# Block layouts in memory, a third weight buffer and a re-timed work order in a two-layer gated MLP with LoRA kernel

## The chip, the cores and the metric

The kernel runs on one NeuronCore of one Trainium2 chip. The metric is the device time of one execution in microseconds, and lower is better. A profiled execution gives a trace of every instruction on five engines: PE (TensorE, with its weight loads as PEld), DVE (VectorE), ACT (ScalarE), POOL (GpSimd) and SP (SyncE, which here only issues transfers).

## The reference, cut to what matters

The input `x` has shape (2, 1024, 256): two samples of 1024 tokens with 256 features. `cond` holds 8 router logits per sample.

```
rw = softmax(cond); w, sel = top_k(rw, 2); w = w / sum(w)       # two experts per sample
mlp(x; g, u, d) = (gelu(x @ g) * (x @ u)) @ d                   # g, u: 256 x 1024, d: 1024 x 256
x = x + sum_k w[k] * mlp(x; expert sel[k]) + mlp(x; shared)
x = x + x @ W_base.T + b_base + 2 * sum_e cond[e] * (x @ As[e].T) @ Bs[e].T
```

All of it is float32. Only the shared MLP and the two chosen experts of each sample are computed. The second layer's low-rank part is folded into one 256 x 256 matrix per sample before it is applied.

## The kernel before, in words

**Precision.** Each float32 operand is split into a rounded part (`hi_of`, a copy to fp32r) and the remainder (`lo_of`, a subtraction). A product is then three matmuls: hi*hi, lo*hi and hi*lo. This document calls the three a *triple*.

**Groups.** The work of the first layer is cut into 24 groups: sample `b` (2), MLP `s` (shared, then the two experts) and quarter `q` of the 1024 hidden columns. A group loads one weight tile `w_raw` of 128 x 1536 floats (768 KB): four gate-and-up blocks A11, A12, A22, A21, then the down weights. Tokens are handled in two blocks of 512. In group 0 the 2 x 2 x 2 block product is done in full (`plain_product`). All later groups use seven products, P1 to P7, instead of eight. The seven need sums of weight blocks (`weight_sum`, S1 to S4, on POOL, into the one buffer `sf`) and sums of `x` blocks (`x_sum`).

**A regular group.** On PE it is 22 triples: seven products each for gate and up, and eight half steps of the down product. PE accumulates in banks `ps_a*` and `ps_d*`. The products share these banks, so a partial result must be copied away before the next product may be added: ACT copies it (`keep`: r1 after P1, u2 after P6, u3 after P7, for g and u), and DVE forms sums from it (`add_part`). The results go through gelu (ACT), `times_up` (DVE), `act_hi` (ACT) and `act_lo` (DVE) into the down product. Meanwhile ACT and POOL prepare the next group's weights: "A hi" and "A1 lo", "A2 lo" (tile `wa`), "S hi" and "S lo" (tile `ws`), "D hi", "D0 lo" and "D1 lo" (tile `wd`).

**Order.** Nothing is scheduled at run time. Every step is entered in a plan with a time (`at`). A regular group's step has the time `REGULAR[name]` plus 22 per group (`reg`); `MOVED` shifts single entries by their number. The plan is sorted by time and issued in that order, so each engine receives its instructions as an in-order queue, and these tables alone decide who stands behind whom.

**Buffers and transfers.** `w_raw` is a ring of two buffers; group g+2 is loaded (`load_w`, plan name "load") into the buffer of group g. Loads of shared weights are issued by SP (L199). Loads of expert weights are indirect transfers issued by POOL (L201), because the row index depends on the router. SP also loads `x` (L253, four blocks of 256 KB per sample, rows of 2 KB that lie 8 KB apart), the first weight tile in four pieces (`load_first`, L210) and the residual (L400), and stores the output (L429). Every load into a buffer has to wait until its last reader is done. In groups 4 and 5 the low-rank matrix is formed in between (`weff_*`, L381), which adds work on POOL and ACT.

**Start.** PE first runs 44 small matmuls (`warm_up`, L437) that depend on no data, then group 0. DVE and ACT split the first `x` blocks and weight pieces as they land. DVE also forms the router's result and `x_sum` 1 to 3. POOL waits for the second weight tile and then begins the sums for group 1.

Of the kernel before, what the change touches and what calls it, by code (L numbers as in the profile page):

```python
# [42 lines left out]
F32 = mybir.dt.float32  # L43
# [7 lines left out]
P = 128  # L51
TB = 512
# [1 line left out]
SCALING = 2.0  # L54
PIECE = 2
REGULAR = {
    "P1g": -1.6, "S1": -1.0, "A hi": -1.0, "r1g": -0.8, "P2g": 1.5, "P1u": 1.8, "P6g": 2.2, "P2u": 2.7,
    "r1 added g": 2.8, "r1u": 3.4, "u2g": 3.6, "S2": 3.6, "gelu 00": 4.5, "P6u": 4.7, "u2u": 5.5,
    "r1 added u": 5.7, "S3": 5.8, "P7g": 8.2, "P5g": 8.4, "S4": 8.5, "act 00": 8.8, "u3g": 8.9,
    "P5g mix": 9.3, "P5u": 11.5, "P7u": 11.6, "S hi": 13.4, "u3 added g": 13.7, "A1 lo": 14.3, "u3u": 14.8,  # L60
    "load": 14.9, "gelu 11": 15.0, "S lo": 15.2, "P4g": 15.4, "u3 added u": 16.0, "act 11": 16.2,
    "P3g": 16.5, "u2 added g": 16.5, "P4u": 16.6, "P3u": 16.6, "hi 00": 16.7, "gelu 10": 17.0,
    "down 00 0": 17.6, "act 10": 19.8, "lo 00": 20.0, "A2 lo": 20.3, "D hi": 20.4, "hi 11": 20.6,
    "u2 added u": 21.9, "gelu 01": 22.3, "lo 11": 22.8, "act 01": 24.9, "hi 10": 25.8, "lo 10": 26.9,
    "down 00 1": 27.8, "down 10 0": 28.2, "down 11 0": 29.0, "D0 lo": 29.7, "down 10 1": 32.0, "hi 01": 32.1,
    "D1 lo": 33.0, "lo 01": 36.9, "down 11 1": 37.3, "down 01 0": 37.6, "down 01 1": 38.3,
}
MOVED = {
    3: -40.0, 16: -9.2, 17: -8.4, 32: -2.9, 33: 3.1, 53: 4.5, 59: 2.8, 60: 3.1, 61: 2.9, 81: 4.9, 86: -35.5,
    99: 4.9, 100: 5.4, 622: -4.7, 1583: 7.7, 1586: 9.9, 1598: 8.0, 1604: 2.6,  # L70
}
WARM = 44
LEN = 22
# [12 lines left out]


@with_exitstack
def moe_then_lora(ctx: ExitStack, tc: tile.TileContext, xT, cond, skill, shared, second, outT):
    nc = tc.nc  # L90
    C, NT = xT.shape
    B, E = cond.shape
    NC = C // P
    G2 = 2 * P
    PW = 4 * G2 + PIECE * C
    NPC = skill.shape[0] // (E * P)
    S = NT // B
    T = S // TB
    assert NC == 2 and T == 2

    sb = ctx.enter_context(tc.tile_pool(name="sb", bufs=1))
# [13 lines left out]
    def const(shape, dtype, name):  # L115
        return sb.tile(shape, dtype, name=name, tag=name)

    raw_ring = Ring(sb, 2, [P, PW], F32, "w_raw")
    wa_ring = Ring(sb, 2, [P, 2, 3 * G2], F32R, "wa")
    sf = const([P, 4 * G2], F32, "sf")  # L120
    ws_ring = Ring(sb, 2, [P, 2, 4 * G2], F32R, "ws")
# [8 lines left out]

    xa = {(b, t): const([P, NC, TB], F32, f"xa{b}{t}") if b < B - 1 else
          raw_ring.tiles[t][:, 0:NC * TB].rearrange("p (c n) -> p c n", c=NC)
          for b in range(B) for t in range(T)}
    bank = {(m, h): pp.tile([P, TB], F32, name=f"ps_{m}{'gu'[h]}", tag=f"{m}{h}")
            for m in "ad" for h in (0, 1)}
    y = [[pp.tile([P, TB], F32, name=f"y{t}{c}", tag=f"y{t}{c}") for c in range(NC)] for t in range(T)]

# [50 lines left out]
    raw, wa, ws, wd = {}, {}, {}, {}  # L188
# [18 lines left out]
    def load_first(lo, hi):  # L207
        if 0 not in raw:
            raw[0] = raw_ring.next()
        nc.sync.dma_start(out=raw[0][:, lo:hi], in_=shared[0:P, lo:hi])  # L210

    def ssum(i):
        return sf[:, i * G2:(i + 1) * G2]
# [34 lines left out]

    xraw, xs = {}, {}

    def load_x(b, k, j, eng=None):
        xraw[b, k, j] = xr_ring.next()
        (eng or nc.sync).dma_start(  # L253
            out=xraw[b, k, j], in_=xT[k * P:(k + 1) * P, (b * T + j) * TB:(b * T + j + 1) * TB]
        )

    def x_sum(b, i, eng):

# [56 lines left out]
    sums, ge, act, acts = {}, {}, {}, {}  # L315
# [32 lines left out]
    def down(g, ij, half):  # L348
# [4 lines left out]
        a, w = acts[g, ij], wd[g]  # L353
        parts = [(n, c) for n in range(3) for c in range(NC)]
        for n, c in parts[:3] if half == 0 else parts[3:]:
# [6 lines left out]
    lora = {}  # L362
    lin = const([P, (2 + NC) * C + B + NC], F32, "lora_in")
    As_sb, BsT_sb, wbT_sb = lin[:, 0:C], lin[:, C:2 * C], lin[:, 2 * C:(2 + NC) * C]
    mix, bias_sb = lin[:, (2 + NC) * C:(2 + NC) * C + B], lin[:, (2 + NC) * C + B:]
# [30 lines left out]
    xres, xas = {}, {}  # L396

    def load_res(b, t, c):
        xres[b, t, c] = xr_ring.next()
        nc.sync.dma_start(out=xres[b, t, c],  # L400
                          in_=xT[c * P:(c + 1) * P, (b * T + t) * TB:(b * T + t + 1) * TB])

    def finish_y(b, t, c):
        nc.vector.tensor_tensor(xa[b, t][:, c, :], y[t][c], xres[b, t, c], ALU.add)
# [20 lines left out]
    def store(b, t, oc, n=slice(0, TB)):  # L425
        r = stores[(b * T + t) * NC + oc][:, n]
        nc.vector.scalar_tensor_tensor(r, outs[b, t, oc][:, n], bias_sb[:, oc:oc + 1],
                                       xa[b, t][:, oc, n], ALU.add, ALU.add)
        nc.sync.dma_start(  # L429
            out=outT[oc * P:(oc + 1) * P, (b * T + t) * TB:(b * T + t + 1) * TB][:, n], in_=r  # L430
        )


    def warm_up():
# [4 lines left out]
    V, A, G = nc.vector, nc.scalar, nc.gpsimd  # L439
# [49 lines left out]
    for n, ij in enumerate(((0, 0), (1, 0), (0, 1), (1, 1))):  # L489
        t = (2, 6, 10, 16)[n]  # L490
# [32 lines left out]
    for g in range(1, NG):  # L523
        if g + 2 < NG:
            reg(g, "load", load_w, g + 2)
        if g + 1 < NG:

            for i in range(4):
                reg(g, f"S{i + 1}", weight_sum, g + 1, i, G)
            reg(g, "S hi", split_ws, g + 1, 0, 4, hi_of, A)  # L530
            reg(g, "S lo", split_ws, g + 1, 0, 4, lo_of, V)
            reg(g, "A hi", split_wa, g + 1, 0, 3, hi_of, A)
# [13 lines left out]
        for ij in blocks:  # L546
            n = "%d%d" % ij
# [54 lines left out]
    b = B - 1  # L602
# [85 lines left out]
```

## Time and profile before

| What | us |
|---|---|
| Median of 3 runs (388.18 to 388.64) | 388.58 |
| The profiled execution's own time | 388.94 |
| Its span, first to last instruction | 387.2 |
| PE busy in the span (1706 matmuls) | 380.0 |
| DVE / ACT / POOL busy | 305.5 / 253.8 / 224.1 |
| First matmul of group 0 starts | 5.38 |
| Last matmul starts | 383.2 |

The span is 1.74 us shorter than the profiled execution's time; that rest lies outside the first and last instruction. The profiled execution is 0.36 us above the median. Matmuls overlap in the pipeline: a matmul of 512 columns is recorded with some 0.39 us, but in an undisturbed stretch they start 0.227 us apart, and a triple takes 0.68 us. The granted clock is 1.000 over the whole span.

### The profile page before, as it was taken

The page shows a single profiled execution, that of the slowest core. Times are in us where ns is not written, and L with a number is a line of the kernel's source. Part 1 is how long each engine was busy: PE and PEld are TensorE (multiplying, and loading weights), DVE is VectorE, ACT ScalarE, POOL GpSimd, SP SyncE. Part 2 cuts the span into 40 slices and gives each one's busy share as a digit, 9 for nine tenths or more (in the row PEclk, how much of TensorE's full clock was granted, in tenths as well). Part 3 has the DMA queues.
Part 4 walks back from the last instruction along what each step waited for, and adds up shares of the span by engine and source line. Part 5 has one row for each costly group of instructions (what it writes and reads, how often), then busy time and mean ns, then how long its engine had stood idle before and what let it go on. Part 6 is the DMA issues. An engine that isn't in the chain of part 4 may idle for free.

```text
span 387.2 us, 4871 instructions
## 1 busy us (share of the span) xinstructions
PE 380.0 (98%) x1706; PEld 313.8 (81%) x1706; DVE 305.5 (79%) x421; ACT 253.8 (66%) x439; POOL 224.1 (58%) x216
## 2 busy tenths in 40 slices
PE   9899999999999999999999999999999999999996
PEld 8677887878888888888888888888888888888885
DVE  4988987797887798988979878777867877777585
ACT  3588876766666677667767876766666775665520
POOL 1667777787866763853834956846747648621000
PEclk9999999999999999999999999999999999999999
DMA  7415202021022202302306022022022021000014
GB/s 208 147 20 226 78 5 81 3 81 50 33 81 81 81 4 81 107 30 108 110 0 190 3 81 81 3 81 81 2 81 82 2 81 48 36 0 0 2 55 163
DMA packets 7832, 26.01 MB, mean 67 GB/s; under 512 B 880, under 2 KB 1664, under 8 KB 7808
## 3 DMA queue, kind: packets, MB, share of 16 engines
q0 software_dynamic: 2336, 12.59, 10.4%
q1 hardware_dynamic: 5472, 13.11, 10.0%
q8 instruction: 13, 0.21, 0.2%
q14 instruction: 11, 0.09, 0.1%
HBM read 23.60 MB, written 2.10 MB: 66 GB/s over the span
## 4 chain that ended last, share of the span: by engine, by line
PE 93%; DVE 2%; DMA 2%; ACT 1%; SPq 1%; issue 0%; ACTq 0%
PE y L358 33%; PE ps_au L289 17%; PE ps_ag L289 17%; PE ps_dg L289 13%; PE ps_du L289 13%; DMA xr<-in_xT 2%; DVE act L334 0%; PE ps_dg L381 0%; SPq L210 0%; DVE wd L183 0%; ACT r_g L313 0%; DVE xr L265 0%; DVE x L183 0%; ACT ws L180 0%; DVE acts L183 0%
## 5 line engine op out<-in xcount | busy, mean ns | idle before, releaser
L358 PE MATMUL y<-acts,wd 128*128 128x512 f32 x576 | 150.3, 389 | 1.3 <-DVE acts L183 1.3
L358 PEld LDWEIGHTS y<-acts,wd 128*128 128x128 f32 x576 | 107.9, 188 | 24.0 <-DVE acts L183 1.7
L222 POOL TENSOR_TENSOR sf<-w_raw 128x256 f32<-128x256 f32 x46 | 37.3, 811 | 106.6 <-DVE ws L183 85.5
L183 DVE TENSOR_TENSOR acts<-act,acts 128x512 fp32r<-128x512 f32 x96 | 75.2, 785 | 14.2 <-ACT acts L180 14.1
L183 POOL TENSOR_TENSOR wa<-w_raw,wa 128x512 fp32r<-128x512 f32 (+1 forms) x46 | 65.1, 1419 | 0.4
L180 ACT CAST acts<-act 128x512 fp32r<-128x512 f32 x96 | 59.4, 619 | 8.2 <-DVE act L336 4.0
L319 DVE TENSOR_TENSOR c_g<-ps_dg,u_g 128x512 f32<-128x512 f32 x46 | 31.7, 690 | 41.6 <-PE ps_dg L289 40.4
L313 ACT COPY u_g<-ps_ag 128x512 f32<-128x512 f32 x46 | 27.0, 588 | 38.0 <-PE ps_ag L289 36.1
L183 POOL TENSOR_TENSOR wd<-w_raw,wd 128x256 fp32r<-128x256 f32 x44 | 43.3, 986 | 9.4 <-ACT wd L180 9.4
L336 DVE SCALAR_TENSOR_TENSOR act<-ge,gate_w,c_u 128x512 f32<-128x512 f32 x48 | 44.6, 929 | 2.9
L328 ACT ACTIVATE ge<-c_g 128x512 f32<-128x512 f32 x69 | 43.8, 634 | 1.7 <-DVE c_g L319 1.7
L289 PE MATMUL ps_ag<-x,ws 128*128 128x512 f32 x138 | 39.0, 391 | 1.3 <-ACT r_g L313 1.3
L289 PE MATMUL ps_au<-x,ws 128*128 128x512 f32 x138 | 38.8, 389 | 0.0
L289 PE MATMUL ps_au<-x,wa 128*128 128x512 f32 x138 | 38.8, 389 | 0.0
L289 PE MATMUL ps_dg<-x,ws 128*128 128x512 f32 x138 | 38.8, 389 | 0.0
L289 PE MATMUL ps_du<-x,ws 128*128 128x512 f32 x138 | 38.7, 389 | 0.0
L289 PE MATMUL ps_ag<-x,wa 128*128 128x512 f32 x138 | 38.7, 389 | 0.0
L313 ACT COPY u_u<-ps_au 128x512 f32<-128x512 f32 x46 | 26.8, 582 | 14.8 <-PE ps_au L289 14.5
L319 DVE TENSOR_TENSOR c_u<-ps_du,u_u 128x512 f32<-128x512 f32 x46 | 31.5, 685 | 2.4 <-ACT u_u L313 2.1
L289 PEld LDWEIGHTS ps_ag<-x,ws 128*128 128x128 f32 x138 | 25.7, 188 | 7.5 <-ACT r_g L313 2.2
L183 DVE TENSOR_TENSOR ws<-sf,ws 128x1024 fp32r<-128x1024 f32 (+1 forms) x24 | 31.3, 1306 | 0.7
L289 PEld LDWEIGHTS ps_au<-x,ws 128*128 128x128 f32 x138 | 25.9, 188 | 5.4
(102 smaller groups left out, 549.7 us busy)
## 6 DMA issues: line engine op xcount, KB each, us to landing
w_raw<-in_shared SPq DMA_DIRECT2D x7, 768.0 KB, 4.4
xr<-in_xT SPq DMA_DIRECT2D x16, 256.0 KB, 4.9
lora_in<-in_second SPq DMA_DIRECT2D x1, 514.0 KB, 5.3
w_raw<-in_shared SPq DMA_DIRECT2D x2, 256.0 KB, 5.7
outT<-u_g SPq DMA_DIRECT2D x2, 256.0 KB, 2.1
outT<-u_u SPq DMA_DIRECT2D x2, 256.0 KB, 2.1
outT<-ge SPq DMA_DIRECT2D x4, 128.0 KB, 1.9
w_raw<-in_shared SPq DMA_DIRECT2D x2, 128.0 KB, 3.3
```

What stands on the lines that cost most here:

```text
L180: (eng.copy if eng is nc.scalar else eng.tensor_copy)(pair[:, 0, :], src)
L183: eng.tensor_tensor(pair[:, 1, :], src, pair[:, 0, :].bitcast(F32), ALU.subtract)
L222: eng.tensor_tensor(ssum(i), a, b, op)
L289: nc.tensor.matmul(ps, lhsT=l, rhs=r, start=(start and n == 0), stop=(n == len(parts) - 1), skip_group_check=True)
L313: nc.scalar.copy(part[m, h], bank["a", h])
L319: nc.vector.tensor_tensor(sums[g, h, ij], bank["d", h], part[m, h], ALU.add)
L328: nc.scalar.activation(ge[g, ij], result(g, 0, ij), AF.Gelu_apprx_tanh)
L336: nc.vector.scalar_tensor_tensor(act[g, ij], ge[g, ij], gate_w[:, s - 1, b:b + 1], result(g, 1, ij), ALU.mult, ALU.mult)
L358: nc.tensor.matmul(y[j][c], lhsT=w[:, wp, o:o + P], rhs=a[:, ap, :], start=first and n == 0, stop=last and n == 2, skip_group_check=True)
```

## The change

The change has four parts.

1. *Layout.* `x` and the output lie in memory as contiguous blocks of 128 x 512 (256 KB each); before, they were cut from a 256 x 2048 matrix. The first weight tile's four pieces lie in memory one behind the other in an array of their own, `piece0`. The numbers and sizes of the transfers stay as they were.
2. *Buffers.* `w_raw` has three buffers. Group g+2 goes into the buffer that group g-1 had.
3. *Order.* All entries of `REGULAR` and most of `MOVED` have new values.
4. *First transfers.* By the new `MOVED` the first weight piece is issued ahead of the first `x` block.

```diff
 REGULAR = {
-    "P1g": -1.6, "S1": -1.0, "A hi": -1.0, "r1g": -0.8, "P2g": 1.5, "P1u": 1.8, "P6g": 2.2, "P2u": 2.7,
-    "r1 added g": 2.8, "r1u": 3.4, "u2g": 3.6, "S2": 3.6, "gelu 00": 4.5, "P6u": 4.7, "u2u": 5.5,
-    "r1 added u": 5.7, "S3": 5.8, "P7g": 8.2, "P5g": 8.4, "S4": 8.5, "act 00": 8.8, "u3g": 8.9,
...
+    "P1g": -3.4, "r1g": -1.5, "A hi": -1.1, "P2g": -0.3, "P1u": -0.2, "r1 added g": 0.6, "P6g": 1.8,
+    "S1": 2.7, "P2u": 3.4, "r1u": 3.9, "P6u": 4.2, "u2g": 4.3, "r1 added u": 4.8, "S2": 5.1, "P5g": 5.5,
+    "gelu 00": 5.8, "S3": 7.1, "S4": 7.1, "A1 lo": 7.1, "u2u": 7.6, "S hi": 9.0, "P7g": 9.1, "u3g": 9.7,
+    "act 00": 10.0, "P5g mix": 10.2, "hi 00": 10.8, "P7u": 11.5, "load": 12.1, "P5u": 12.5,
...
+    "lo 11": 19.1, "hi 10": 22.8, "D hi": 23.8, "down 00 1": 23.8, "lo 10": 24.3, "down 10 0": 25.3,
...
+    "lo 01": 34.6, "down 01 0": 35.2, "down 01 1": 35.6, "D0 lo": 36.0, "D1 lo": 40.8,
 }
 MOVED = {
-    3: -40.0, 16: -9.2, 17: -8.4, 32: -2.9, 33: 3.1, 53: 4.5, 59: 2.8, 60: 3.1, 61: 2.9, 81: 4.9, 86: -35.5,
-    99: 4.9, 100: 5.4, 622: -4.7, 1583: 7.7, 1586: 9.9, 1598: 8.0, 1604: 2.6,
+    20: -0.2, 37: 2.4, 38: 2.9, 39: 3.5, 45: -4.1, 74: -1.8, 80: -1.5, 81: 2.7, 86: -35.0, 89: 2.2, 99: 8.1,
+    100: 3.7, 1583: 5.5, 1598: 4.3, 1604: 4.6,
 }
...
-    raw_ring = Ring(sb, 2, [P, PW], F32, "w_raw")
+    raw_ring = Ring(sb, 3, [P, PW], F32, "w_raw")
...
-        nc.sync.dma_start(out=raw[0][:, lo:hi], in_=shared[0:P, lo:hi])
+        nc.sync.dma_start(out=raw[0][:, lo:hi], in_=piece0[lo * P:hi * P].rearrange("(p c) -> p c", p=P))
...
-        (eng or nc.sync).dma_start(
-            out=xraw[b, k, j], in_=xT[k * P:(k + 1) * P, (b * T + j) * TB:(b * T + j + 1) * TB]
-        )
+        nc.sync.dma_start(out=xraw[b, k, j], in_=x[b, j, k])
...
-        nc.sync.dma_start(
-            out=outT[oc * P:(oc + 1) * P, (b * T + t) * TB:(b * T + t + 1) * TB][:, n], in_=r
-        )
+        nc.sync.dma_start(out=outT[b, t, oc][:, n], in_=r)
...
-        "xT": np.ascontiguousarray(np.asarray(x).reshape(B * S, C).T),
+        "x": np.ascontiguousarray(np.asarray(x).reshape(B, T, TB, NC, P).transpose(0, 1, 3, 4, 2)),
...
+        "piece0": np.concatenate([shared[0, :, lo:hi].reshape(-1) for lo, hi in
+                                 ((0, G2), (G2, 2 * G2), (2 * G2, 4 * G2), (4 * G2, shared.shape[2]))]),
```

The residual load changes as `load_x` does (`in_=x[b, t, c]`). What the new tables do to the queues, where this document speaks of it:

- ACT, start: before, the casts of `x` for P5 and P6 and of two activations stood ahead of the first half of "S hi", and then came the gelu of block 11; now this order is: cast for P5 (`x_76`), `act_hi` of block 01, cast for P6 (`x_75`), first half of "S hi", gelu of block 11.
- DVE, start: the remainder of the first activation (`acts` block 00) now stands before the remainder of `wd`; before, it stood behind it and behind `x_sum` 2.
- PE, group 0: both halves of down 00 now come before the two plain products of block 11, and both halves of down 10 between P1g and P2g of group 1.
- ACT, every group: r1g now stands ahead of "A hi"; before, "A hi" stood ahead of r1g. Then come hi 10, "D hi" and r1u.
- POOL, every group: the load stands ahead of "D0 lo" and "D1 lo"; before, it stood behind them.

## The prediction, made before the changed kernel was run

> **What bounds the kernel now.** I read the windows view first: the busy time of each engine by stage, to see where PE is not full.
>
> ```profile
> 0.00:13.00 13.00, 12.23 (x76) 10.86 (x77) 7.26 (x15) 6.05 (x12) 1.51 (x7) 1.00 0.66 202
> 13.00:25.00 12.00, 10.63 (x46) 8.13 (x45) 11.10 (x22) 7.72 (x16) 7.93 (x7) 1.00 0.20 67
> 60.00:100.00 40.00, 38.67 (x174) 31.29 (x173) 32.71 (x39) 26.79 (x48) 30.36 (x29) 1.00 0.19 60
> 100.00:367.00 267.00, 267.00 (x1180) 221.08 (x1179) 209.61 (x286) 181.88 (x313) 156.70 (x149) 1.00 0.17 56
> ```
>
> The columns are PE, PEld, DVE, ACT, POOL. From 100 to 367 us PE is busy for 267.00 of 267 us, and triples follow each other at 0.68 us: nothing is to be had there, only lost. What can be had lies in the first 100 us. The chain of waits in order of time shows the places, because its steps should be 0.68 us apart:
>
> ```profile
> 65.37 0.68 PE ps_dg L289 x3
> 66.05 0.69 PE ps_au L289 x3
> 67.36 0.97 PE ps_ag L289 x3
> 68.33 0.69 PE ps_du L289 x3
> ...
> 82.86 0.71 PE ps_au L289 x3
> 84.25 0.96 PE ps_ag L289 x3
> ```
>
> From 66.05 to 67.36 it is 1.31 us, so 0.63 too much, and the next triple takes 0.97, so 0.29 too much: 0.9 us (the refill after a stop is about 0.11 of it). I took the starts of all matmuls in the trace and subtracted 0.227 us each. Left over are: at 14.75 us 1.56 (with refill), at 21.6 0.35, at 36.9 0.14, at 66.3 0.90, at 81.6 0.15, at 83.2 0.98. Sum 4.08 us: the ceiling of what order and buffers can give, unless PE starts earlier.
>
> *The first stall* (timeline of the start):
>
> ```profile
> 12.57 2.10 POOL L222 TENSOR_TENSOR sf<-w_raw 128x256 f32<-128x256 f32 x2 [10.31 <-DMA w_raw<-in_shared]
> 12.85 1.23 DVE L183 TENSOR_TENSOR wd<-w_raw,wd 128x512 fp32r<-128x512 f32 x1
> 14.00 1.23 DVE L265 TENSOR_TENSOR xr<-xr,xr 128x512 f32<-128x512 f32 x1
> 15.15 1.21 DVE L183 TENSOR_TENSOR acts<-act,acts 128x512 fp32r<-128x512 f32 x1
> 16.42 0.73 PE L358 MATMUL y<-acts,wd 128*128 128x512 f32 x2 [1.29 <-DVE acts L183]
> ```
>
> PE waits for the first activation's remainder, which is third in DVE's queue. The same DVE operations take 0.68 us before POOL begins at 12.57 and 1.2 afterwards: they start 0.60 apart alone and 1.15 beside POOL.
>
> *The two stalls of the low-rank groups* (first the timeline of POOL):
>
> ```profile
> 59.92 1.90 POOL L201 DMA_INDIRECT w_raw<-in_skill,idx  x1 [0.16 <-POOL wa L183]
> ```
>
> and the timeline of ACT:
>
> ```profile
> 65.99 0.83 ACT L180 CAST wa<-w_raw 128x768 fp32r<-128x768 f32 x1 [2.84 <-DMA w_raw<-in_skill,idx]
> 66.73 0.58 ACT L313 COPY r_g<-ps_ag 128x512 f32<-128x512 f32 x1
> ```
>
> The expert's weights are issued at 59.92 and land at 65.9. ACT's "A hi" waits for them, and r_g stands behind it on ACT. PE's P6g waits for r_g. At 82.9 it is the same. The list of waits confirms both causes:
>
> ```profile
> ACT wa L180 <- DMA w_raw<-in_skill,idx: 4.0, 2, 2.8
> PE ps_ag L289 <- ACT r_g L313: 1.3, 2, 0.7
> PE y L358 <- DVE acts L183: 1.3, 1, 1.3
> ```
>
> **Third buffer and r1g ahead of "A hi".** In a regular group the load no longer needs group g's D lo to be done. In POOL's new order it follows A1 lo, which needs "A hi", and that comes 1.4 to 2.2 us after the group's first product starts. So the load is issued some 4 us into a group. By the rows above it takes 1.9 plus about 4.2 us and has landed by 10 to 11 us, 4 us before the next group (14.96 us = 22 x 0.68) begins. In group 4 POOL first waits for the low-rank copy (about 7.6 us in) and adds L389 (1.3), so the load lands about 15 us in; the group is 15.7 long with L381, and "A hi" needs it 1.4 us after that. In addition r_g no longer stands behind that cast. So 0.90 and 0.98 go, from two causes, each enough by itself. The small one at 81.6 came from a DVE operation of 2.83 us beside four POOL operations in a row (0.15); with POOL's queue reordered I count it as gone. Sum -2.03.
>
> **Start of PE: nothing.** The 44 warm-up matmuls follow at 0.105 us from 0.77 and end at 5.38, exactly when group 0 starts; their number stays. The first piece now goes ahead of x, but both were there by 4.5 us (ACT's first cast 4.54, DVE's 4.23). If x comes 0.3 us later its cast still ends at 5.0.
>
> **The start's new order, worked through with before's landings.** DVE: act 00 at 10.45, x_sum 3 at 11.04, acts lo at 11.80 (ACT's cast ends at 11.78), P3's remainder at 12.4, then beside POOL wd's remainder 13.0 to 14.2. PE needs that at 14.51 (the third matmul of down 00, which starts at 14.06): the stall of 1.56 goes. What is late next: x_sum 1 at 14.15, act 10 at 15.3 to 15.95. PE now runs the whole of down 00 first and wants the bank that act 10 reads at 15.65: stall 0.37 + 0.11 = 0.48. Then the router (1.1 us on DVE, from 18.00 to 19.12 in the trace), acts lo 17.0, act 01 18.1, x_sum 2 18.7 to 19.4. ACT's cast for P6 waits for that and starts at 19.45, half of "S hi" at 19.97, and only then the gelu of block 11, 20.5 to 21.1. PE wants the bank it frees for P2g at 18.63 + 3 x 0.68 = 20.67: stall 0.48 + 0.11 = 0.59. So behind PE's wait stand P1u, P6g and all the rest. Before, P2g came at 22.04 after the same number of matmuls; now at 21.15. r_u on ACT then ends at 24.75 against 24.65 wanted: 0.15. From there to 40 us my steps along the queues leave each product 0.5 us or more, so the 0.14 at 36.9 goes. In group 2 the exp and gelu tables (3.0 us on ACT, 38.48 to 41.47 in the trace) now stand ahead of u2g, which then ends at 41.25 where PE wants P7g at 41.2: 0.10.
>
> So this part removes 1.56 + 0.35 + 0.14 = 2.05 and adds 0.48 + 0.59 + 0.15 + 0.10 = 1.32: -0.73.
>
> Here the Trainium skill is weighed, *SBUF — State Buffer*, "SBUF: two separate sides": the port pair of DVE and POOL is an exclusive lock, and the loser is blocked for the other's whole instruction. A POOL operation of 256 columns takes 0.74 us alone (66.05), so by the rule a DVE operation behind one would come every 0.60 + 0.74 = 1.34 us; the trace has 1.15. With 1.34 act 10 would be 0.4 us later and the first new stall 0.9 instead of 0.48. I take 1.15, which was measured at this very place.
>
> **Layout: nothing at the centre.** For it speaks the list of DMA issues:
>
> ```profile
> w_raw<-in_shared SPq DMA_DIRECT2D x7, 768.0 KB, 4.4
> xr<-in_xT SPq DMA_DIRECT2D x16, 256.0 KB, 4.9
> ```
>
> A third of the bytes takes longer. But most x blocks were issued in fours behind each other. In the packet records a 2 KB packet takes 84 ns at the median; in the first 10 us 764 of them have some 28 us more in all, because single ones take up to 551. Over 16 engines that is 1.8 us: the most that contiguous blocks can bring forward the landing of the second weights (12.5). But the contiguous 6 KB rows have such packets too (median 234 ns, mean 291 from 13 to 22 us), so the layout may not be their cause: lower bound nothing. The skill, *DMA: Bandwidth & Descriptors*, "Latency and other measured facts", has power-of-two row pitches slow at 2 MiB (164 GB/s) and above; at 512 KiB it has 207, near full. Here the pitch is 8 KiB, so by the rule nothing is gained; by the packets up to 1.8 us of landing. And an earlier landing of the second weights starts POOL earlier, beside more of DVE's queue: with x 1.4 us and POOL 1.7 us earlier, act 10 comes at 16.3 instead of 15.95, and P2g again at about 21.1. I take 0, range -1 to +0.4. Stores: the last one lands 1.5 us after its issue with 1 KB packets of 47 ns; same packets after, at most -0.2.
>
> **Regular groups: nothing, by cover.** With steps of ACT at 0.5 us (casts of 768 columns 0.74), r_g starts at 0.88 us, A hi 1.36, hi 10 2.1, D hi 2.6, r_u 3.1 to 3.7; P6u wants it at 7 x 0.68 = 4.76. Cover 1.0 us. P6g wants r_g (ends 1.47) at 2.04. D0 lo is wanted at 14.05 and done by about 7. DVE's sums each have 1 us or more.
>
> **Sum.** -2.03 - 0.73 = -2.76, about -2.8: 388.94 - 2.8 = 386.1 for a profiled execution. The one shown lies 0.36 above the median, so against the median 388.58 I predict 385.8.
>
> **Rivals.**
> - *The layout pays*: landings come forward without the collision, and the new stalls close too. The whole 4.08 goes: 384.5. For it: x at 9.35 us holds DVE for 0.72. Against: the pitch, and POOL. Chance 0.14.
> - *The start only moves its stalls*: DVE is busy 11.10 of 12 us from 13 to 25 in any order. The start gains nothing or loses up to 1: 386.6 to 387.6, or below 0.2% of gain if the low-rank stalls return in part. Chance 0.22 (0.15 faster, 0.07 same).
> - *The third buffer's load gets in the way*: SP can now issue the third weights at about 5 us instead of 14. If their packets mix with the second's (768 KB, 2.7 us at the 286 GB/s of the packet records from 30 to 36 us), POOL starts at up to 15.2 and A1 lo of group 1 (done 5.0 us after POOL's start by its rows, wanted at 18.9) is 1.3 us late: 387.1, up to 388 with what hangs on it. For: all share 16 engines. Against: one queue, landings in order of issue in the trace. Chance 0.06. (The buffers' part not happening is excluded: SP's new queue has the load into a third tile.)
> - *Slower*: a wait in every regular group. ACT's r_u has cover 1.0 us; if hi 10 or "A hi" ahead of it is late by more, P6u stops. Price: 0.2 us over the cover costs 0.31 with refill, times 22 groups = 6.8, minus 2.8 gained: 392.6. It decides from 1.0 us of lateness on; break-even is 0.13 us per group. Chance 0.08.
>
> **Numbers.** The main case has 0.50, range 385.2 to 386.6. A measurement of this kernel can tell 0.2% (0.78 us) from no change. Faster by more: 0.50 + 0.14 + 0.15 + 0.04 = 0.83; within: 0.07 + 0.02 + 0.01 = 0.10; slower: 0.07. The range goes from the ceiling (384.5) to a gain of 1 (387.6).
>
> **What would show it.** Right: matmul starts of 0.68 per triple through groups 4 and 5, and the indirect transfers landing about 4 us ahead of "A hi"; no stop at 14.75, small ones near 15.7 and 20.7; group 0 at 5.38. Wrong: idle PE between 100 and 367 us (the slower rival); P2g of group 1 not before 22 us (start only moved); POOL's first operation well before 11 us (layout) or after 13.5 (mixing).

## The result and the profile after

The changed kernel took 386.26 us (median, 385.94 to 386.7) against 388.61 us of the kernel before, run beside it: a ratio of 0.9942, interval 0.993 to 0.9954. The gain is 2.35 us; 2.8 were forecast, and 385.8 was predicted. The profiled execution is the fastest of its kernel, 385.94 us with a span of 384.2, so between the two profiled executions the gain is 3.00 us.

The windows view of the kernel after, with the same columns (PE, PEld, DVE, ACT, POOL, then the granted clock):

```profile
0.00:13.00 13.00, 12.23 (x75) 10.79 (x76) 7.56 (x15) 6.26 (x12) 2.64 (x8) 1.00 0.79 263
13.00:25.00 12.00, 12.00 (x52) 9.17 (x51) 11.97 (x25) 8.13 (x16) 7.71 (x7) 1.00 0.45 154
60.00:100.00 40.00, 39.63 (x181) 32.61 (x180) 33.93 (x39) 27.56 (x49) 32.94 (x32) 1.00 0.13 40
100.00:364.00 264.00, 264.00 (x1166) 218.63 (x1165) 217.88 (x283) 178.55 (x309) 137.01 (x146) 1.00 0.17 56
```

From 13 to 25 us PE now has work in all of the 12 us (10.63 before), and DVE is fuller still: 11.97 of 12 us (11.10 before). From 60 to 100 us only 0.37 us is idle (1.33 before). From 100 to 364 us PE is full, as before: the new order costs the regular groups nothing. Since matmul records overlap, stops of 0.1 or 0.2 us do not show in the busy time; the starts of the matmuls, further below, show them.

The list of waits is the short form of the same. Columns: who waited for whom, us in total, times, longest. Of the old entries for `r_g` (1.3 us) and for `acts` (1.3 us) none is left on PE; the first entry is the wait before the first warm-up matmul:

```profile
PE y L431 <- PEq L676: 0.8, 1, 0.8
PE ps_dg L286 <- DVE c_g L316: 0.4, 1, 0.4
```

The remaining wait of 0.4 us is found in the chain of waits at 79.5 us, where the triple after it takes 0.96 instead of 0.68:

```profile
79.54 0.69 DVE c_g L316
80.22 0.04 issue
80.27 0.96 PE ps_dg L286 x3
```

**One balance for all kernels.** I took the starts of all matmuls in each trace and added up what lies between neighbours beyond 0.227 us. The last matmul starts at the first one's start plus these sums plus 373.1 to 373.3 us (373.5 in r1g_first and two_buffers), so little else moves the end of PE. The sums of 4 to 8 us include spacing at half speed (see below). "Tail" is the span less the last start. The columns 4–8 to 100–365 are stretches of the span in us. Stops of 0.08 us from 8 to 14 us in layout_only and lora_moved have no column.

| Kernel | median us | ratio to before (interval) | first matmul | 4–8 | 14–30 | 30–60 | 60–100 | 100–365 | last starts | tail |
|---|---|---|---|---|---|---|---|---|---|---|
| before | 388.61 | | 5.38 | 0.50 | 1.91 | 0.14 | 2.03 | 0 | 383.20 | 4.0 |
| after | 386.26 | 0.9942 (0.993–0.9954) | 5.38 | 0.72 | 0.60 | 0 | 0.64 | 0 | 380.58 | 3.6 |
| layout_only | 389.1 | 1.0014 (1.0008–1.0021) | 5.32 | 1.42 | 1.64 | 0 | 1.73 | 0 | 383.34 | 3.8 |
| order_and_buffers | 387.13 | 0.9958 (0.9944–0.9972) | 6.10 | 0.15 | 1.72 | 0 | 0.64 | 0 | 381.86 | 3.7 |
| r1g_first | 387.19 | 0.9964 (0.9951–0.9977) | 5.03 | 0.69 | 1.81 | 0.15 | 0.23 | 0 | 381.46 | 3.9 |
| three_buffers | 388.79 | 1.0004 (0.9995–1.0012) | 5.04 | 0.79 | 1.91 | 0.15 | 1.71 | 0 | 382.76 | 3.9 |
| load_early | 391.35 | 1.0078 (1.0058–1.0098) | 5.38 | 0.59 | 1.77 | 1.08 | 0 | 2.91 | 384.87 | 3.9 |
| two_buffers | 395.72 | 1.0174 (1.0157–1.0192) | 4.84 | 1.06 | 0.57 | 0 | 7.56 | 2.66 | 390.18 | 3.8 |
| r1g_behind | 386.14 | 0.9931 (0.9918–0.9944) | 5.38 | 0.66 | 0.82 | 0 | 0.64 | 0.15 | 380.86 | 3.6 |
| lora_moved | 385.58 | 0.9918 (0.9904–0.9931) | 5.08 | 1.63 | 0.56 | 0 | 0 | 0 | 380.56 | 3.6 |
| start_freed | 385.9 | 0.9917 (0.9904–0.993) | 5.00 | 1.68 | 0 | 0.37 | 0.64 | 0 | 380.84 | 3.6 |
| logits_late | 384.92 | 0.9908 (0.9892–0.9923) | 4.89 | 0.69 | 0 | 0 | 0.65 | 0 | 379.32 | 3.6 |
| all_freed | 384.8 | 0.9892 (0.9878–0.9907) | 5.38 | 0.71 | 0 | 0.27 | 0 | 0 | 379.46 | 3.6 |
| layout_logits_late | 387.27 | 0.9969 (0.9957–0.9981) | 5.07 | 0.64 | 0.53 | 0.26 | 2.15 | 0 | 381.81 | 3.8 |

The sums belong to the one profiled execution, the medians to all of them. Where two kernels' intervals overlap, the difference of their medians is no more than a hint unless the executions themselves lie apart. Between before and after the balance closes: 4–8 us +0.22, 14–30 us -1.31, 30–60 us -0.14, 60–100 us -1.39, tail -0.38; together -3.00. Of the tail's -0.38 the layout alone gives 0.17 (3.96 to 3.79 in layout_only); the rest was not traced.

Names: "block 10" of `x` is the second `x` transfer, features 128 to 255 of the first 512 tokens; act, hi and lo with a block number are `times_up`, `act_hi` and `act_lo` of that block.

### The profile page after: what moved, and what is told of

It is laid out like the page before. It is cut to its first block, busy times and chain, and to the rows that moved or that the text cites. A ratio compares the mean times of both kernels' runs of the same rounds, so it can differ in the third digit from the quotient of the medians.

```text
span 384.2 us, 4886 instructions
## 1 busy us (share of the span) xinstructions
PE 379.7 (99%) x1706; PEld 314.2 (82%) x1706; DVE 315.8 (82%) x421; ACT 252.6 (66%) x439; POOL 206.6 (54%) x216
## 3 DMA queue, kind: packets, MB, share of 16 engines
q1 hardware_dynamic: 5472, 13.11, 9.8%
## 4 chain that ended last, share of the span: by engine, by line
PE 97%; DVE 2%; issue 1%; DVEq 0%
PE y L355 33%; PE ps_au L286 17%; PE ps_ag L286 17%; PE ps_dg L286 13%; PE ps_du L286 13%; PE y L431 1%; PE ps_ag L306 1%; PE ps_au L306 1%; PE ps_du L306 1%; PE ps_dg L306 1%; DVE act L333 1%; PE ps_dg L378 0%; DVE c_g L316 0%; DVE ws L182 0%; DVE c_u L316 0%
## 5 line engine op out<-in xcount | busy, mean ns | idle before, releaser
L355 PE MATMUL y<-acts,wd 128*128 128x512 f32 x576 | 153.8, 389 | 0.0
L182 DVE TENSOR_TENSOR acts<-act,acts 128x512 fp32r<-128x512 f32 x96 | 83.3, 869 | 6.1 <-ACT acts L179 5.8
L182 POOL TENSOR_TENSOR wa<-w_raw,wa 128x512 fp32r<-128x512 f32 (+1 forms) x46 | 52.3, 1136 | 31.0 <-ACT wa L179 22.6
L316 DVE TENSOR_TENSOR c_g<-ps_dg,u_g 128x512 f32<-128x512 f32 x46 | 31.7, 689 | 35.5 <-ACT u_g L310 19.4
L333 DVE SCALAR_TENSOR_TENSOR act<-ge,gate_w,c_u 128x512 f32<-128x512 f32 x48 | 49.1, 1023 | 2.8
L182 POOL TENSOR_TENSOR wd<-w_raw,wd 128x256 fp32r<-128x256 f32 x44 | 40.1, 930 | 11.5 <-ACT wd L179 11.0
L325 ACT ACTIVATE ge<-ps_ag 128x512 f32<-128x512 f32 x25 | 14.9, 597 | 33.1 <-PE ps_ag L286 32.5
L286 PEld LDWEIGHTS ps_dg<-x,ws 128*128 128x128 f32 x138 | 25.9, 188 | 5.5
```

Of the source, the lines that this page charges most:

```text
L182: eng.tensor_tensor(pair[:, 1, :], src, pair[:, 0, :].bitcast(F32), ALU.subtract)
L286: nc.tensor.matmul(ps, lhsT=l, rhs=r, start=(start and n == 0), stop=(n == len(parts) - 1), skip_group_check=True)
L316: nc.vector.tensor_tensor(sums[g, h, ij], bank["d", h], part[m, h], ALU.add)
L325: nc.scalar.activation(ge[g, ij], result(g, 0, ij), AF.Gelu_apprx_tanh)
L333: nc.vector.scalar_tensor_tensor(act[g, ij], ge[g, ij], gate_w[:, s - 1, b:b + 1], result(g, 1, ij), ALU.mult, ALU.mult)
L355: nc.tensor.matmul(y[j][c], lhsT=w[:, wp, o:o + P], rhs=a[:, ap, :], start=first and n == 0, stop=last and n == 2, skip_group_check=True)
```

## The experiments

The theory to be tested: the gain is 2.03 us from the low-rank groups, by two causes (the third buffer and r1g), 0.73 us from the start's order, and nothing from the layout. The rivals: the layout does it, or only one of the two causes does.

### The layout and the rest, taken apart

layout_only is the kernel before with the block layouts of `x`, output and first weights; order_and_buffers is the kernel after with the old ones.

```diff
# layout_only: before, with
+        nc.sync.dma_start(out=raw[0][:, lo:hi], in_=piece0[lo * P:hi * P].rearrange("(p c) -> p c", p=P))
+        nc.sync.dma_start(out=xraw[b, k, j], in_=x[b, j, k])
...
# order_and_buffers: after, without these
```

> The kernel before with the block layouts of x, output and first pieces alone; orders and two buffers as before. Theory (order and buffers bring the gain): the stop of PE near 14.75 us stays at 1.0 to 1.6 us, those near 66 and 83 us stay at 0.9 and 1.0; only the stores at the end are shorter, so the time falls by 0.0 to 0.5 us against before. Rival (the layout pays): x and first weights land 1 us or more earlier, DVE is ahead, the stop near 14.75 us shrinks below 0.6, and the time falls by 1 us or more.

> The changed kernel with the old layouts (x cut from the 256 x 2048 matrix, first pieces cut from the weight tile's rows). Theory: it keeps nearly all, 1.8 to 2.6 us below before, with stops of PE under 0.4 us each near 15.7 and 20.4 and the 0.6 near 79.5. Rival (the layout pays): 1 us or less below before, since the new order of the start counts on early landings and its stops near 15.7 and 20.7 grow to 0.5 and more each.

Measured: the layout alone is 0.5 us slower (389.1), which neither side expected. Order and buffers alone give 387.13, 1.5 us below before and between the two expectations, so beside them the layout is worth 0.87 us in the medians. The intervals of order_and_buffers and after just overlap, but all five executions of the one (386.77 to 387.38) lie above all four of the other (385.94 to 386.7). The layout's worth is not one number: its sign depends on what else is done.

Alone, the first blocks land early, but `x` block 10 lands later (7.52 us, in before 6.58), and PE waits for it. The list of waits of layout_only:

```profile
PE y L354 <- DVE acts L181: 1.4, 1, 1.4
PE ps_ag L305 <- DVE x L178: 1.2, 1, 1.2
PE ps_ag L285 <- ACT r_g L309: 1.0, 2, 0.6
```

The wait of 1.2 us for `x` is new; the other two are before's. In exchange later stops shrink a little, as the one near 83 us does by 0.28: PE comes to it 0.43 us later, but the transfer that it hangs on lands only 0.14 us later. And the tail is 0.2 us shorter: its stores land 2.0 and 1.7 us after issue, against 2.1 and 1.9.

Without the layout, the new order has a start that is far from the one I worked out. The waits of order_and_buffers, in its profiled execution, which is the slowest of its five:

```profile
PE ps_dg L289 <- ACT ge L328: 0.7, 1, 0.7
PE ps_ag L309 <- DVE x L180: 0.5, 1, 0.5
PE ps_dg L289 <- DVE c_g L319: 0.4, 1, 0.4
PE ps_du L309 <- DVE act L334: 0.3, 1, 0.3
```

The first `x` block lands at 5.50 us (3.64 in after, 4.21 in before), the third at 9.87 (8.14 in after) and the second weights at 13.11 (11.38 and 12.50). DVE's and ACT's queues run 0.6 to 1.3 us later than in after, and the stops at the start sum up to 1.72 us instead of 0.60. DVE's timeline in order_and_buffers shows one more loss, an operation on 2 columns that takes 1.09 us while POOL is busy (0.39 us in after):

```profile
16.71 1.09 DVE L156 TENSOR_TENSOR gap<-top 128x2 f32<-128x2 f32 x1
```

### The two causes of the low-rank stalls, one by one, from before

```diff
# r1g_first
-    ... "A hi": -1.0, "r1g": -0.8, ...
+    ... "A hi": -1.0, "r1g": -1.1, ...
# three_buffers
-    raw_ring = Ring(sb, 2, [P, PW], F32, "w_raw")
+    raw_ring = Ring(sb, 3, [P, PW], F32, "w_raw")
# load_early: three_buffers, and
-    "load": 14.9, ...
+    "load": 7.6, ...
```

> The kernel before with one number changed: r1g at -1.1, so that ACT's copy r_g stands ahead of the cast A hi in every group. Theory (each cause enough by itself): the transfer still lands at 65.9 and 82.8, the cast still waits for it, but P6g no longer waits: the stops near 66 and 83 us go, the time falls by 1.6 to 2.0 us. Rival (only the earlier landing helps, because what stands behind the cast is then late: gelu and r_u): the stops move to P6u and less than 0.6 us is gained.

> The kernel before with a third weight buffer and nothing else. Theory (POOL's queue, not the buffer, holds the load back: before shows the issue waiting 0.16 us for POOL's own cast and no longer): the indirect loads are issued near 59.9 and 76.8 us as before, the stops near 66 and 83 us stay, the time is within 0.4 us of before. Rival (the buffer was what held it): the stops go, 1.5 to 2 us less.

> The kernel before with three weight buffers and the load ahead of D0 lo in POOL's queue (plan time 7.6 instead of 14.9); r1g stays behind A hi. Theory: the two transfers land 3 us or more earlier, A hi waits no more, the stops near 66 and 83 us go, the time falls by 1.6 to 2.0 us. Rival (the landing was not the bound, POOL or ACT would be late anyway): less than 0.6 us.

*r1g_first* gives 1.4 us with one number, a little less than the 1.6 to 2.0 expected. ACT's timeline, to be held against before's, where the cast stands ahead of `r_g` and ends its wait for the load:

```profile
65.14 0.59 ACT L313 COPY r_g<-ps_ag 128x512 f32<-128x512 f32 x1 [2.26 <-PE ps_ag L289]
65.73 0.84 ACT L180 CAST wa<-w_raw 128x768 fp32r<-128x768 f32 x1
```

`r_g` now runs when PE has its product ready, at 65.14 instead of 66.73, and the windows row of this kernel has no idle PE at all in this stretch:

```profile
60.00:100.00 40.00, 40.00 (x182) 32.82 (x181) 33.91 (x40) 27.81 (x51) 32.94 (x31) 1.00 0.19 60
```

*three_buffers* changes nothing (388.79). POOL's timeline says why: the load is issued at 59.82 us, in before at 59.92. Not the buffer holds it back but its place in POOL's queue:

```profile
57.90 1.76 POOL L183 TENSOR_TENSOR wa<-w_raw,wa 128x512 fp32r<-128x512 f32 x1
59.82 1.89 POOL L201 DMA_INDIRECT w_raw<-in_skill,idx  x1 [0.16 <-issue]
```

*load_early* moves it forward: the loads land at 56.2 and 71.6 us. The stops near 66 and 83 are gone, without r1g being touched, and yet the kernel is 2.8 us slower. New stops stand at 46.0, 104.3 and 144.7 us; the largest is 2.39 us. DVE's and POOL's timeline there:

```profile
141.57 0.74 DVE L336 SCALAR_TENSOR_TENSOR act<-ge,gate_w,ps_au 128x512 f32<-128x512 f32 x1
142.23 4.32 DVE L183 TENSOR_TENSOR acts<-act,acts 128x512 fp32r<-128x512 f32 x1
141.95 0.75 POOL L183 TENSOR_TENSOR wd<-w_raw,wd 128x256 fp32r<-128x256 f32 x1
142.65 0.74 POOL L222 TENSOR_TENSOR sf<-w_raw,sf 128x256 f32<-128x256 f32 x1
143.33 0.73 POOL L183 TENSOR_TENSOR wd<-w_raw,wd 128x256 fp32r<-128x256 f32 x1
144.03 1.97 POOL L183 TENSOR_TENSOR wa<-w_raw,wa 128x512 fp32r<-128x512 f32 x2
```

The DVE operation takes 0.68 us when it is alone. Here POOL runs five operations without a pause from 141.95 to 146.00, and DVE ends at 146.55: it was shut out over all of them. A run without a pause is not enough for that, though. In before, where the load stands behind them, the same operations also follow one another, from 141.43 to 146.33, and DVE gets its turns: its operations with two SBUF inputs take 0.68 to 1.18 us there, and POOL's 1.18 and 1.30 instead of 0.74 (DVE, then POOL):

```profile
143.29 0.68 DVE L183 TENSOR_TENSOR acts<-act,acts 128x512 fp32r<-128x512 f32 x1
142.13 1.18 POOL L222 TENSOR_TENSOR sf<-w_raw,sf 128x256 f32<-128x256 f32 x1
143.28 1.30 POOL L183 TENSOR_TENSOR wd<-w_raw,wd 128x256 fp32r<-128x256 f32 x1
```

So in the old order the early load removed both stalls and cost more than it gained, by a shut-out whose trigger is not known.

### The same two causes, one by one, from after

```diff
# two_buffers
-    raw_ring = Ring(sb, 3, [P, PW], F32, "w_raw")
+    raw_ring = Ring(sb, 2, [P, PW], F32, "w_raw")
-    "load": 12.1, ...
+    "load": 19.0, ...
# r1g_behind
-    "P1g": -3.4, "r1g": -1.5, "A hi": -1.1, ...
+    "P1g": -3.4, "r1g": -1.5, "A hi": -1.6, ...
```

> The changed kernel with two weight buffers; the load then has to stand behind D1 lo (plan time 19.0 instead of 12.1). Theory (r1g ahead of A hi suffices, and the order of the start does not need the third buffer): within 0.5 us of the changed kernel, so 1.8 to 2.8 us below before; the transfers land about 3 us later. Rival (the third buffer carries the gain in groups 4 and 5): stops of 0.5 to 1 us each at P6u in these groups, 1 to 2 us slower than the changed kernel.

> The kernel after with one number changed: the split of the first weights on ScalarE (A hi) due at -1.6 in place of -1.1, so that it stands ahead of the copy r1g on ScalarE's queue in each regular group. Theory: three buffers and the early load make A hi ready some 4 us before its place, so that r1g behind it is late by one ScalarE copy at most: the stops near 66 and 83 stay away (below 0.2 us each) and the time is within 0.4 us of the kernel after (385.9 to 386.7), which says that each of the two edits removes those stops by itself. Rival: r1g's place is what removes them: then stops of 0.5 us or more come back near 66 and 83, and further ones in the other 14 groups, and the time is 387.5 or more.

*two_buffers* has r1g ahead of "A hi" and still loses 9.5 us to after. Its load stands behind the last reader of the second buffer on POOL ("D1 lo", 18.8) and is issued at 80.45 us; the timeline of ACT and PE:

```profile
81.44 0.59 ACT L310 COPY r_g<-ps_ag 128x512 f32<-128x512 f32 x1 [1.30 <-PE ps_ag L286]
85.85 0.83 ACT L179 CAST wa<-w_raw 128x768 fp32r<-128x768 f32 x1 [3.82 <-DMA w_raw<-in_skill,idx]
86.58 0.61 ACT L179 CAST acts<-act 128x512 fp32r<-128x512 f32 x1
87.25 1.65 PE L355 MATMUL y<-acts,wd 128*128 128x512 f32 x3 [3.13 <-ACT acts L179]
```

`r_g` is in time. But "A hi" waits 3.82 us for the transfer, and the cast of an activation for the down product ("hi 10") stands behind it on ACT; PE waits 3.13 us for that, and 6.9 us at three such places together by the list of waits. So r1g's place removes the wait only for r1g itself: whatever else follows "A hi" inherits the wait. In the order of after, the third buffer is needed.

*r1g_behind* is the counterpart: 386.14 us, within the 0.4 us of after that the first theory expected. ACT's timeline at the place of before's second stop:

```profile
80.93 0.82 ACT L179 CAST wa<-w_raw 128x768 fp32r<-128x768 f32 x1
81.66 0.57 ACT L310 COPY r_g<-ps_ag 128x512 f32<-128x512 f32 x1
82.13 0.62 ACT L179 CAST acts<-act 128x512 fp32r<-128x512 f32 x1
```

The cast waits for nothing (the transfer landed at 77.6), `r_g` is late by that one cast, and no stop follows. Only in group 1, with its short start, does it cost something: `r_g` ends at 22.42 there, and a stop of 0.32 us stands at 22.0. In after, r1g's place is worth nothing measurable in the time (386.14 against 386.26); it is the early load that counts.

### The stop at 79.5 us

In after, "lora_W" and "lora_B" are split on POOL in one run with the next group's weights. lora_moved gives the split a later place.

```diff
-    at(t0 + 15.5, weff_split, b, lo_of, G)
+    at(t0 + 29.15, weff_split, b, lo_of, G)
```

> The changed kernel with the remainder of the low-rank weights (128 x 512 on POOL) moved from between lora_B's remainder and D1 lo to behind A1 lo of the next group. Theory (DVE's operation of 4.24 us at 75.4 was shut out by POOL operations that follow each other without a pause, and PE waits for what stands behind it): the operation takes less than 3 us, the stop of 0.64 us near 79.5 falls below 0.2, the time is 0.4 to 0.7 us below the changed kernel. Rival (DVE waits for something else, or the run of POOL stays long enough without this one operation): the stop stays above 0.4 us.

The timeline of after, DVE and then POOL:

```profile
75.38 4.24 DVE L333 SCALAR_TENSOR_TENSOR act<-ge,gate_w,c_u 128x512 f32<-128x512 f32 x1
79.54 0.68 DVE L316 TENSOR_TENSOR c_g<-ps_dg,u_g 128x512 f32<-128x512 f32 x1
75.25 0.47 POOL L372 TENSOR_SCALAR sbf<-lora_in 128x256 f32<-128x256 f32 x1
75.70 1.28 POOL L182 TENSOR_TENSOR lora_W<-wef,lora_W 128x512 fp32r<-128x512 f32 x1
76.94 0.73 POOL L182 TENSOR_TENSOR lora_B<-sbf,lora_B 128x256 fp32r<-128x256 f32 x1
77.64 0.73 POOL L182 TENSOR_TENSOR wd<-w_raw,wd 128x256 fp32r<-128x256 f32 x1
78.33 0.72 POOL L221 TENSOR_TENSOR sf<-w_raw 128x256 f32<-128x256 f32 x1
```

It is the same shut-out as in load_early: DVE gets in at the first break of POOL's run, at 79.05, and PE's P3g waits for the sum behind it. In lora_moved POOL pauses from 76.38 to 76.91, and DVE gets its turn (DVE, then POOL):

```profile
76.04 0.88 DVE L333 SCALAR_TENSOR_TENSOR act<-ge,gate_w,c_u 128x512 f32<-128x512 f32 x1
76.91 0.74 POOL L182 TENSOR_TENSOR lora_B<-sbf,lora_B 128x256 fp32r<-128x256 f32 x1 [0.52 <-ACT lora_B L179]
```

The stop of 0.64 us is gone from the balance; the median falls by 0.68 us to 385.58, as expected, though the intervals of the two kernels touch. The profiled execution, at 385.94, doesn't show the gain in its end: it had a stop of 1.5 us at 6.3 us, since `x` block 10 landed at 7.48 us.

### The start: DVE's queue or the transfers?

In after, DVE does the router's work (1.34 us, from 15.84 to 17.18) and the second sum of `x` early. The 16 packets of the logits go out among those of the first weights and `x`. logits_late moves the operations and the transfer behind the start, start_freed the operations only, layout_logits_late is layout_only with the transfer and the router moved, and all_freed is logits_late with lora_moved.

```diff
# start_freed
-    at(11.0, x_sum, 0, 1, V)
-    at(11.5, router)
+    at(11.2, x_sum, 0, 1, V)
+    at(36.0, router)
# logits_late: start_freed, and
-    at(-29.1, router_load)
+    at(20.8, router_load)
# all_freed: logits_late, and
-    at(t0 + 15.5, weff_split, b, lo_of, G)
+    at(t0 + 29.15, weff_split, b, lo_of, G)
# layout_logits_late: layout_only, and
+    at(20.8, router_load)
+    at(36.0, router)
```

> The changed kernel with three edits of the start: x_sum 1 behind act 10 on DVE, the router's eight DVE operations moved to group 1 (plan time 36), and the logits' transfer issued by POOL after the sums of group 1 instead of at 1.3 us. Theory for DVE: the stops near 15.7 (0.19), 20.4 (0.26) and 24.1 us (0.15) go. Theory for the transfers (the logits' 16 packets meet the first blocks, whose packets then take up to 1.9 us): no packet above 1 us in the first 8 us, the second first piece lands before 5 us instead of 5.97 and the first x block of the second half before 6.3 instead of 6.79, the 0.2 us of later start go. Together 0.5 to 1.0 us below the changed kernel. Rival (the held packets come from the blocks' own addresses): the second piece still lands at 5.5 us or later.

> The kernel after with the second sum of x after, and the router's work far behind, the first operations of VectorE; the transfer of the logits stays at the start. Theory A (the logits' transfer itself slows the weights and x at the start; the operations on VectorE cost little): the stops at 15.7, 20.4 and 24.1 shrink by the VectorE time taken out, at most 0.3 us together, packets of over 1 us stay in the first 8 us, and the time is 385.8 to 386.1, so that most of the 1.3 us that logits_late gained is the transfer's. Theory B (VectorE's order is what counts): the stops at 15.7, 20.4 and 24.1 go as in logits_late, and the time is 385.0 to 385.4.

> The kernel before with x, output and first weights in contiguous blocks (as layout_only), and with the logits' transfer and the router's work moved behind the start. Theory: layout_only lost time because the blocks arrive in the same 3 us as the logits' 16 packets and were held by them; without them no packet of the first 8 us lasts over 1 us, the stop near 6.5 us of 1.34 us shrinks below 0.5 us, and the time is 387.2 to 388.2 (ratio 0.996 to 0.999). Rival: the loss is in the order of this kernel's start (VectorE and TensorE wait for what comes later, however early the first pieces land): the stop near 15 us stays at 1.5 us or more and takes up what came free, and the time is 388.8 or more.

> The kernel after with both edits together: the low part of the lora weights split later on GpSimd (due 29.15 in place of 15.5), and the logits' transfer, their use and the second sum of x moved out of the start. Theory: the two gains lie at different places (a stop of 0.64 us near 79.5, and the stops at 15.7, 20.4 and 24.1 of 0.60 us together), so they add. logits_late gave 384.92 with the stop near 78 still there at 0.65, so this kernel comes to 384.2 to 384.5, ratio to the kernel before 0.988 to 0.990, with no stop over 0.2 us after 13 us. Rival: TensorE's regular stretch has no slack to take the gain up and the lora split only moves its run of GpSimd work beside another VectorE operation: then a stop of 0.4 us or more stands near 88 to 95 and the time stays at 384.8 to 385.1.

*logits_late*: 384.92 us, 1.3 less than after and more than the 0.5 to 1.0 expected. The stops at 15.7, 20.4 and 24.1 are gone. The sum from 4 to 8 us, which should have fallen, did not (0.69 against 0.72): PE began 0.49 us earlier and then waited 0.52 us at 6.1 us. *start_freed* has the three stops gone too, with the transfer left early. That PE is late there (1.68 us lost by 8 us) does not explain it, since lora_moved is as late and keeps 0.56 us of them. So these three, 0.60 us together, are DVE's queue, and theory B is right on them. On the time theory A is right: the median is 385.9. But the interval overlaps that of logits_late, so what the transfer alone costs is not firmly shown. The five executions are 384.98, 384.99, 385.9, 386.21 and 386.24, so it lands now at one end, now at the other. The profiled one (386.21) shows what the slower ones have, and the waits end on `x`:

```profile
6.22 0.40 PE L306 MATMUL ps_au<-x,wa 128*128 128x512 f32 x1
7.97 0.47 PE L306 MATMUL ps_ag<-x,wa 128*128 128x512 f32 x1 [1.36 <-DVE x L179]
```

Here `x` block 10 landed at 7.38 us. Over the kernels with the new layout: where the logits' transfer is early, the second weight piece lands at 5.3 to 6.5 us and block 10 at 6.6 to 7.5 (after, layout_only, two_buffers, start_freed, r1g_behind, lora_moved); where it is late, at 4.0 to 4.5 and 6.3 to 6.7 (logits_late, all_freed, layout_logits_late). So the transfer delays the piece that stands next to it; for block 10 the two ranges overlap. With the old layout and the same early transfer the piece lands at 4.9 to 5.9 us.

How it does is not settled. I expected packets of over 1 us to vanish with it. In after the logits' packets of 512 bytes take up to 1.17 us, with 27 ns for the undisturbed ones, and 2 KB packets beside them up to 1.9 us instead of 84 ns. In logits_late no packet of the first 8 us reaches 0.77 us. But in layout_logits_late two take 1.0 and 1.2 us, and in all_freed some up to 1.8 us, with no logits beside them.

*layout_logits_late*: 387.27 us, 1.8 under layout_only and 1.3 under before. The stop near 6.5 shrinks from 1.34 to 0.47, and the one near 15 from 1.64 to 0.53. The number is as expected, though long packets remain. Since this kernel moves the router too, the part of the stop near 15 may be DVE's. The old layout with the transfer and the router late was not run, so the 1.3 us under before are not shown to be the layout's. Its 16 executions reach from 386.13 to 388.93, the widest spread of all, and why is open.

*all_freed*: 384.8 us, the best median of all, but only 0.12 below logits_late instead of the 0.4 to 0.7 expected. In its profile the stop near 79 is gone as expected (-0.65), a new one of 0.27 us at 43.6 takes part of it, and this execution's matmuls come 0.5 us later from the first one on (5.38 against 4.89). That last goes with the speed of the warm-up matmuls, point 8 below. Against after its interval (0.9878 to 0.9907) lies wholly below (0.993 to 0.9954): about 1.5 us faster. Against logits_late the intervals overlap.

## Why the prediction was right, and where its steps were not

The time (385.8 against 386.26), the sign and the stage were right. The sum was right partly by luck, because two steps that were off nearly cancel: in the profiled pair "third buffer and r1g" gave -1.39 and not -2.03, and the start 14–60 us with 4–8 us gave -1.23 and not -0.73. The tail adds -0.38, of the -0.2 at most that I gave the stores and had set at 0 at the centre.

1. **The two large stalls: right.** The 1.88 us at 66.3 and 83.2 are gone, and the indirect loads land at 59.98 and 77.68 us, 4.7 and 3.6 us ahead of "A hi" (64.71 and 81.31), where about 4 was forecast.
2. **"From two causes, each enough by itself": half right.** r1g_first and load_early remove the stops each alone, and r1g_behind shows that the early load alone is enough in after. But three_buffers shows that a buffer is no early load, and two_buffers that r1g alone is not enough in the new order, because "hi 10" stands behind "A hi" too.
3. **"The small one at 81.6 I count as gone": the mis-sized term.** It did not go, it grew from 0.15 to 0.64 us, at 79.5. I had named the cause, POOL operations in a row beside DVE, and assumed that a new queue on POOL is a better one. Now five operations stood in a row while DVE waited, and its operation took 4.24 us instead of 2.83. With 0.64 in place of 0 this term alone makes the -2.03 a -1.39.
4. **The start, stop by stop.** The order of the new stops was right, the sizes less: forecast 0.48, 0.59, 0.15 and 0.10; measured 0.19 at 15.7, 0.26 at 20.4, 0.15 at 24.1, none at 41. The first is smaller since the start itself was 0.22 later, so that PE asked later: act 10 ran from 15.24 to 15.92 where 15.3 to 15.95 was forecast. The second is smaller because DVE's `x_sum` 2 ended at 19.07 and not at 19.4: ACT's gelu ended at 20.73, forecast 21.1.
5. **"Layout: nothing at the centre": wrong, and with it "worked through with before's landings".** The landings of before don't hold in the new order. In order_and_buffers, with the old layout, the first `x` block landed 1.3 us later than before and the second weights 0.6 us later, and the stops from 14 to 30 us sum up to 1.72 us, not the 1.22 (0.48 + 0.59 + 0.15) worked out. With group 0 beginning 0.72 us later its start gains nothing over before. So the -0.73 forecast for the order of the start was earned only together with the layout, which had been put at nothing. The layout brings the second weights forward from 13.11 to 11.38: 1.73 us, what I had set as the most (1.8). In the old order it is 0.45 us only (12.50 to 12.05), so this depends on the order too. I then argued that this would set POOL beside more of DVE's queue and be worth nothing (P2g "again at about 21.1"). P2g came at 20.8, and the layout was worth 0.87 us here. Alone it cost 0.5 us: the range of -1 to +0.4 held the one, and nearly the other. The argument from the row pitch, drawn from far larger pitches, did not settle the case.
6. **The rule weighed.** The row's 1.15 us per DVE operation beside POOL held in this place:

```profile
12.95 1.22 DVE L182 TENSOR_TENSOR wd<-w_raw,wd 128x512 fp32r<-128x512 f32 x1
14.10 1.22 DVE L260 TENSOR_TENSOR xr<-xr,xr 128x512 f32<-128x512 f32 x1
15.24 0.68 DVE L331 TENSOR_TENSOR act<-ge,ps_du 128x512 f32<-128x512 f32 x1
```

   With 1.34, by the Trainium skill's rule in *SBUF — State Buffer*, "SBUF: two separate sides", act 10 would have come at 15.6. But a number for the pair does not exist: 60 us later one such operation took 4.24 us. The long case fits the page's "exclusive lock", but its "for the whole instruction" is too little there: the loser was shut out over five instructions of the other engine, in after and in load_early.
7. **The regular groups: right.** No stop from 100 to 364 us.
8. **The start of PE.** "5.38, unchanged" held for the two profiled executions, but other kernels begin their group 0 between 4.84 and 5.38 us with the same 44 warm-up matmuls (order_and_buffers, at 6.10, waits for `x`). PE's timeline of after, and of logits_late:

```profile
3.28 2.34 PE L431 MATMUL y<-const-bfloat16-1.0 128*128 128x128 bf16 x20
5.38 0.78 PE L306 MATMUL ps_ag<-x,wa 128*128 128x512 f32 x1
5.95 0.63 PE L306 MATMUL ps_au<-x,wa 128*128 128x512 f32 x1
6.38 0.51 PE L306 MATMUL ps_ag<-x,wa 128*128 128x512 f32 x1
```

```profile
3.28 1.80 PE L431 MATMUL y<-const-bfloat16-1.0 128*128 128x128 bf16 x20
4.88 0.48 PE L306 MATMUL ps_ag<-x,wa 128*128 128x512 f32 x1
```

   The last 20 warm-up matmuls take 2.34 us or 1.80, and the first real ones 0.78, 0.63 and 0.51 us instead of 0.39: PE gets to full speed earlier or later. In logits_late the step lies within the warm-up, whose matmuls stand 0.107 us apart at first and 0.059 at the end; in after all 20 stand 0.107 apart. The granted clock of the windows (1.00 in both) doesn't show this. The Trainium skill, *TensorE: Matmul & The Clock Gate*, "Part 1: The HAM clock gate", has it that PE starts at half speed and is let go by a window that runs free of the kernel's start, some 500 ns either way, run by run. The 4.84 to 5.38 us agree with that. A gain of 0.3 us that hangs on the start can be told only over several executions.

Of the rivals, "the layout pays" had a true core, and "the start only moves its stalls" was seen in order_and_buffers (1.91 to 1.72). The third buffer's load did not get in the way: it was issued at 5.12 us, and the second weights still landed at 11.38, ahead of it. The slower rival was not seen in after, but two_buffers shows how it looks: a wait on ACT with the cast of an activation behind it.

## What to carry to other kernels

When an engine's queue is in order, ask of each waiting instruction not only who waits for it but who stands behind it: in the old order one number in a table was worth 1.4 us, and a third buffer alone nothing, since the place in the queue set the issue. Landings are part of the order: the stalls of a re-ordered start can't be worked out with the old kernel's landings, and a layout must be judged beside the order it will run with, as it cost 0.5 us in one and gained 0.9 us in the other. Look at POOL's unbroken runs beside VectorE operations that read two tiles of SBUF, above all where PE's next product hangs on one. Most such runs did no harm here, but where one did, a single break in it undid the shut-out of 4.24 us.

## What the runs showed of the hardware

- VectorE's operations with two SBUF inputs can be shut out by a run of five GpSimd operations in a row: 4.24 us in after, 4.32 us in load_early, against about 0.7 alone. Beside other runs the two engines took turns, 1.15 us a step in after's start, and beside the run at 141.4 us of before VectorE's took no more than 1.18. Long shut-outs are rare: of some 200 operations of 128 x 512 with two SBUF inputs in after, this one alone took more than 2.5 us. What decides was not found.
- A stop of PE can cost more than its length. After two_buffers' stop of 3.41 us at 83.7, PE ran at half speed; the windows row (the clock, 0.50, stands behind the five engines):

```profile
87.00:92.00 5.00, 4.75 (x11) 3.83 (x12) 3.56 (x4) 2.72 (x7) 4.68 (x5) 0.50 0.00 0
```

  Eleven matmuls in 5 us: they stand 0.427 us apart instead of 0.227. Of that kernel's 9.5 us some 2.4 us are this (12 matmuls by 0.2). Stops of 2.64 us in the same kernel (at 105.5) and of 2.39 us in load_early were not followed by this, and no stop of after or before was longer than 1.6.
- The 16 packets of the logits' transfer, 512 bytes each, and 2 KB packets beside them took up to 1.17 and 1.9 us in after, against medians of 27 and 84 ns in before, where the same transfer's packets took 88 ns at most. With the new layout the weight piece issued next landed at 5.3 to 6.5 us, and at 4.0 to 4.5 where the transfer was moved. The mechanism is open, since single packets of 1 to 1.8 us also came without that transfer.
